# First sequence: when GpSimd rotates k and q, and where blocks of the second layer's weights and the split of k stand in the queues

## The chip, the cores and the metric

The kernel runs on one core of a Trainium2 chip. A core has a matrix engine (TensorE, PE in the profile, with its weight loads as PEld), VectorE (DVE), ScalarE (ACT) and GpSimd (POOL); SyncE (SP) issues most transfers. Each engine works through its own queue in order and waits on semaphores for what others produce. The metric is the device time of one execution, in microseconds; less is better.

## The reference

For eight sequences of 512 rows and 256 columns, with `xn` the layer norm of `x`:

```python
xn = _layernorm(x)
s = attention(xn, in_proj_w, out_proj_w)   # 16 heads of 16, rotary embedding on q and k,
                                           # causal, no further back than 250 positions
h = concatenate([xn, -xn])                 # 512 columns
h = 2 * relu(s0 * (h @ sign(k0)))          # to 1024; sign: True is 1, False is -1
h = 2 * relu(s1 * (h @ sign(k1)))          # to 1024
h = s2 * (h @ sign(k2))                    # to 256
x = x + s * silu(h)
```

The weights of the three layers come as booleans, one byte each; k1 is 1024 x 1024.

## The kernel before, in words

**Work and tiles.** Everything is computed transposed, with the 512 positions of a sequence along the free axis. The two layers take the eight blocks ("units") of 128 features one after the other. To keep precision with fast matrix formats, the input, h1 and h2 are each held as a high half in float16 (ScalarE, L529) and a low half (VectorE, L527: the PSUM result less the high half); a unit's matmuls run over all high blocks and then over all low ones. The PSUM tiles of the units come from a pool of three (`ps_m`), so that a unit can start when the low half of the unit three before it is written. The weights are made from the bytes on the chip: for the second layer a block is one of eight groups of 128 output features, once as float16 (`w1h`) and once as float32 (`w1l`). `make_w1` does it, on ScalarE (L192) or GpSimd (L194). Its source `kb1` is one transfer of 1 MB, which ScalarE's queue issues at 4.33 us and which lands at about 14.7 us.

**q and k.** `project` multiplies the normed input by the weights of q or k, in a part "a" and a part "b" of 512 positions each. VectorE multiplies each by cosine and sine (L404), two instructions to a part; the products of part "b" lie in a tile `m_b` of one buffer, those of "a" in one of two. `rotate` (L425) combines them on GpSimd, two instructions. `split_hi` rounds the result on ScalarE (L442) and sends it to DRAM; `split_lo` takes the rest on VectorE (L449) and sends it too (L435). `stack` (L457) reads them back in the layout of the scores, for a group of four heads at a time: one load for k and two for q. SP issues all of these transfers. The high half lies in one buffer (`hi`).

**v.** `project_v` multiplies for v in four pieces, whose PSUM tiles come from the pool of two that q's projections use before them and the scores behind them (`ps_s`); ScalarE copies each into `v_pad` (L372).

**The order.** `run` is a planner written in the kernel. Each piece of work has a place (`at`) and a cost in planner's units; the pieces are taken by place, and a clock adds up their costs. What follows a piece (the evictions, the rotation, the splits) has a delay, and is issued before the first piece at which the clock has reached its due time. An engine's queue has its instructions in the order of issue. Pieces with a negative place come first. In the first sequence the clock stands at 2.74 before place 0. The halves of k's a and b then cost 0.87 each (to 4.48), q's a and b 1.75 each (to 7.98), the units of the first layer 0.87 each. So k's b products are due at 4.48, q's b products at 7.98 + 1.5 = 9.48, unit 0's eviction at 8.85 and unit 1's at 9.72, the low halves 0.6 later, and v0's copy at 10.59. `rotate` is due 1.4 behind the b products; `hi_after` and `lo_after` (L401) are the delays of `split_hi` and `split_lo` from the same point. A weight block has cost 0 and is issued at its place.

**Downstream.** Behind the first layer come the units of the second layer (eight of them, each in two parts); the first step of the scores stands between units 1 and 2, and then follow steps of exponentials (ScalarE, L752), masks (GpSimd, L768 and L775) and values. The other seven sequences use the same functions with their own places.

Of the kernel before, what the change touches and what calls it, by code (L numbers as in the profile page):

```python
# [34 lines left out]
def tile_attention_times_gated_ffn(  # L35
# [42 lines left out]
    nc = tc.nc  # L78
# [109 lines left out]
    def make_w1(f, p, engine):  # L188

        w, k = w1[p][:, :, ts(f, P)], kb1[:, :, ts(f, P)]  # L190
        if engine is nc.scalar:
            nc.scalar.activation(w, k, AF.Identity, bias=sgnn[:, 1:2], scale=sgn2[:, 1:2])  # L192
        else:
            engine.tensor_scalar(w, k, sgn2[:, 1:2], sgnn[:, 1:2], ALU.mult, ALU.add)  # L194
# [180 lines left out]
    def project(b, what, part, half=None):  # L375

        st = states[b]
        col = E * "qk".index(what) + P * "ab".index(part)
        if b == 0 and what == "q":
            ps = ps_s.tile([P, 2, T], F32, tag="sc", name=f"{what}{part}_ps_{b}")[:, 0]  # L380
        elif half == 1:
            ps = st.pop(part)
        else:
            ps = ps_m.tile([P, T], F32, tag="mm", name=f"{what}{part}_ps_{b}")
            st[part] = ps
        for cols in [slice(0, T)] if half is None else [ts(half, T // 2)]:
            for c in range(EC):
                nc.tensor.matmul(
                    ps[:, cols], wqkv_sb[:, c, ds(col, P)], st["xT"][:, c, cols],
                    start=(c == 0), stop=(c == EC - 1),  # L390
                )
        if half == 0:
            return

        m = turned.tile(
            [P, 2, T], F32, tag=f"m{part}", name=f"m_{what}{part}_{b}",
            bufs=2 if part == "a" else 1,
        )
        st[what, part] = m

        hi_after, lo_after = (4.0, 5.1) if b else (4.5, 5.7) if what == "k" else (5, 6.2)  # L401

        def times(i):
            nc.vector.tensor_tensor(  # L404
                m[:, i], ps, rope_sb[:, i if part == "a" else 1 - i], ALU.mult
            )

        def both():
            times(0)
            times(1)  # L410
            if part == "b":
                return [
                    (1.4, lambda: rotate(b, what)),
                    (hi_after, lambda: split_hi(b, what)),
                    (lo_after, lambda: split_lo(b, what)),
                ]


        return [(1.5 if b == 0 and what + part == "qb" else 0.0, both)]

    def rotate(b, what):
        st = states[b]
        m, n = st[what, "a"], st.pop((what, "b"))
        for i, op in enumerate((ALU.subtract, ALU.add)):
            nc.gpsimd.tensor_tensor(m[:, i], m[:, i], n[:, i], op)  # L425
# [13 lines left out]
    def split_hi(b, what):  # L439
        st = states[b]  # L440
        hi = st["hi"] = turned.tile([P, 2, T], F32R, tag="hi", name=f"{what}h_{b}")
        nc.scalar.copy(hi, st[what, "a"])  # L442
        to_dram(b, what, 0, hi)

    def split_lo(b, what):
        st = states[b]
        m = st.pop((what, "a"))
        lo = m.bitcast(F32R)
        nc.vector.tensor_tensor(lo, m, st["hi"].bitcast(F32), ALU.subtract)  # L449
        to_dram(b, what, 1, lo)  # L450
# [9 lines left out]
    def prepare(b, plain=False):  # L460
# [26 lines left out]
        for what in "kq":  # L487
            for n, part in enumerate("ab"):
                if b == 0 and what == "k" and not plain:

                    out += [
                        (-34.3 if n == 0 else -32.95, 0.87, lambda p=part: project(b, "k", p, 0)),
                        (at["k"] + dp * n, 0.87, lambda p=part: project(b, "k", p, 1)),
                    ]
                else:
                    out.append((
                        at[what] + dp * n, 1.75, lambda w=what, p=part: project(b, w, p),
                    ))
# [497 lines left out]
            (-32.9 if c == 0 else -32.6, 0, lambda c=c: make_w0l(c)),  # L996
        ]
    for w, f, at, engine in (
        ("l", 0, -20, nc.gpsimd), ("l", 1, -19, nc.gpsimd), ("l", 2, 5.1, nc.gpsimd),
        ("h", 0, -17, nc.scalar), ("h", 1, -16, nc.scalar), ("h", 2, 5.2, nc.gpsimd),  # L1000
        ("l", 3, 11.8, nc.gpsimd), ("l", 4, 11.9, nc.gpsimd), ("l", 5, 12.0, nc.gpsimd),
        ("l", 6, 19.3, nc.gpsimd), ("l", 7, 19.4, nc.gpsimd), ("h", 3, 15.2, nc.scalar),
        ("h", 4, 17.0, nc.scalar), ("h", 5, 18.7, nc.scalar), ("h", 6, 20.4, nc.scalar),
        ("h", 7, 22.2, nc.scalar),
    ):
        everything.append((at, 0, lambda f=f, w=w, e=engine: make_w1(f, w, e)))
# [141 lines left out]
```

## Time and profile before

| | us |
|---|---|
| median of 3 runs | 611.47 |
| lowest and highest | 610.42, 612.76 |
| the profiled execution | 612.91 |
| its span | 611.2 |

Mean clock of TensorE in the profiled execution: 0.991 of full speed. Busy shares of the span: PE 98%, PEld 60%, DVE 63%, POOL 50%, ACT 48%; the 16 DMA engines moved 122 GB/s in the mean. Lists of instructions give: start (us), duration (us), engine, source line, operation, output<-inputs, shape, and in brackets the idle time before it and what ended that. Neighbouring instructions of one kind are merged ("x2"), and the duration is then of all. Tables by stretch give the stretch and its length, then the busy time of PE, PEld, DVE, ACT and POOL, the granted clock of TensorE, the DMA engines' mean busy share and GB/s. The rows of the page with 40 digits show tenths in 40 equal slices of the span.

### The profile page before, as it was taken

What the parts mean: (1) busy time and instruction counts of PE and PEld (TensorE: products, weight loads), DVE (VectorE), ACT (ScalarE), POOL (GpSimd) and SP (SyncE); (2) the same over time, 40 slices, a digit from 0 to 9 for tenths busy, and PEclk for the clock granted to TensorE, in tenths of its full rate; (3) what the DMA queues carried; (4) which work ended last, traced back from release to release, by engine and by line L of the source; (5) the groups of instructions that cost most, each with busy time, mean ns of one, the idle gap of its engine ahead of it and who ended that gap; (6) DMA issues with size and microseconds to landing.
All of it is one profiled execution on the core that took longest, in us unless ns stands there. A gap on an engine that the chain in (4) does not pass through costs nothing. (4 is left out here: it accounts for less than half of the span.)

```text
span 611.2 us, 11176 instructions
## 1 busy us (share of the span) xinstructions
PE 596.9 (98%) x4492; PEld 367.7 (60%) x4492; DVE 384.2 (63%) x606; ACT 295.1 (48%) x414; POOL 308.0 (50%) x368
## 2 busy tenths in 40 slices
PE   7899999999999999999999999999999999999994
PEld 5465565556665556555566566655565556667783
DVE  6654736556675584665856658566676557654774
ACT  4576654435544545545354454543554445555421
POOL 2855542346524665336634357245572446627642
PEclk9799999999999999999999999999999999999998
DMA  9371732216322263314333252432533216212201
GB/s 286 144 242 53 276 122 86 87 70 229 117 87 87 97 215 104 120 55 180 131 104 122 79 218 73 148 112 80 207 101 123 89 69 241 70 54 75 83 1 41
DMA packets 38061, 74.51 MB, mean 122 GB/s; under 512 B 5360, under 2 KB 13040, under 8 KB 38000
## 3 DMA queue, kind: packets, MB, share of 16 engines
q1 hardware_dynamic: 35568, 71.48, 34.0%
q10 hardware_dynamic: 2432, 2.23, 1.1%
q8 instruction: 37, 0.61, 0.4%
q14 instruction: 24, 0.20, 0.1%
HBM read 44.30 MB, written 29.39 MB: 121 GB/s over the span
## 5 line engine op out<-in xcount | busy, mean ns | idle before, releaser
L752 ACT ACTIVATE p<-sc 128x1024 f32<-128x1024 f32 (+2 forms) x144 | 138.3, 1013 | 75.5 <-PE sc L733 45.8
L768 POOL TENSOR_SCALAR_AFFINE_SELECT p<-p 128x512 f32<-128x512 f32 x128 | 91.1, 718 | 126.6 <-ACT p L752 126.5
L518 PE MATMUL h_ps<-h1l,w1l_sb 128*128 128x512 f32 (+1 forms) x576 | 146.2, 396 | 0.0
L518 PE MATMUL h_ps<-h1h,w1h_sb 128*128 128x512 f16 (+1 forms) x576 | 123.1, 356 | 0.0
L518 PEld LDWEIGHTS h_ps<-h1l,w1l_sb 128*128 128x128 f32 x576 | 100.2, 188 | 29.5 <-issue 9.2
L529 ACT ACTIVATE h2h<-h_ps 128x512 f16<-128x512 f32 (+1 forms) x72 | 39.5, 548 | 112.3 <-PE h_ps L518 112.3
L518 PEld LDWEIGHTS <-w1h_sb 128*128 128x128 f16 x576 | 51.2, 98 | 58.7 <-issue 17.3
L775 POOL TENSOR_SCALAR_AFFINE_SELECT p<-p 128x512 f32<-128x512 f32 (+1 forms) x96 | 49.7, 517 | 70.9 <-ACT p L752 67.4
L807 PE MATMUL po<-p,v_pad 128*32 128x378 f32 (+4 forms) x1216 | 76.7, 372 | 0.1
L633 DVE RECIPROCAL den<-den 128x256 f32<-128x256 f32 (+1 forms) x32 | 52.5, 1644 | 24.9 <-POOL den L628 24.9
L527 DVE SCALAR_TENSOR_TENSOR h2l<-h_ps,h2h 128x512 fp32r<-128x512 f32 (+1 forms) x72 | 43.7, 608 | 30.9 <-ACT h2h L529 30.9
L733 PEld LDWEIGHTS sc<-q,k 32*128 32x128 f32 x1216 | 44.0, 184 | 29.4 <-issue 21.5
L527 DVE SCALAR_TENSOR_TENSOR h1l<-h_ps,h1h 128x512 fp32r<-128x512 f32 x64 | 42.8, 680 | 29.4 <-ACT h1h L529 29.4
L884 DVE RECIPROCAL S<-S 128x128 f32<-128x128 f32 x64 | 57.5, 920 | 0.1
L733 PE MATMUL sc<-q,k 32*128 32x378 f32 (+4 forms) x1216 | 57.4, 306 | 0.1
L518 PE MATMUL h_ps<-xl,w0l_sb 128*128 128x512 f32 x128 | 53.7, 501 | 0.0
L807 PEld LDWEIGHTS po<-p,v_pad 128*32 128x32 f32 x1216 | 31.7, 109 | 28.7 <-issue 16.6
L529 ACT ACTIVATE h1h<-h_ps 128x512 f16<-128x512 f32 x64 | 38.1, 598 | 22.1 <-PE h_ps L518 22.1
L518 PE MATMUL h_ps<-xh,w0h_sb 128*128 128x512 f16 x128 | 39.8, 393 | 1.1 <-DVE h1l L527 1.1
L301 DVE TENSOR_TENSOR xT<-xT,of_all 128x512 f32<-128x512 f32 x28 | 22.7, 815 | 26.4 <-DMA of_all<-d 26.0
L572 PE MATMUL z_ps<-h2l,w2l_sb 128*128 128x512 f32 (+1 forms) x144 | 36.1, 391 | 0.2 <-DVE h2l L527 0.2
L365 PE MATMUL v_ps<-wqkv_sb,xT 128*128 128x256 f32 x128 | 33.8, 387 | 1.6 <-ACT v_pad L372 1.6
(101 smaller groups left out, 721.5 us busy)
## 6 DMA issues: line engine op xcount, KB each, us to landing
q<-dq SPq DMA_DIRECT2D x64, 256.0 KB, 3.4
dq<-qh SPq DMA_DIRECT2D x16, 512.0 KB, 3.2
dq<-m_qa SPq DMA_DIRECT2D x16, 512.0 KB, 5.5
k<-dk SPq DMA_DIRECT2D x32, 256.0 KB, 2.7
dk<-kh SPq DMA_DIRECT2D x8, 512.0 KB, 3.6
dk<-m_ka SPq DMA_DIRECT2D x8, 512.0 KB, 2.6
x<-in_x_dram SPq DMA_DIRECT2D x30, 128.0 KB, 2.8
xT<-in_x_t_dram SPq DMA_DIRECT2D x7, 512.0 KB, 5.3
```

What stands on the lines that cost most here:

```text
L365: nc.tensor.matmul(v.rearrange("p n s d -> p (n s d)"), st["xT"][:, c, ts(t, P)], wqkv_sb[:, c, 2 * E :], start=(c == 0), stop=(c == EC - 1),)
L518: nc.tensor.matmul(ph, w[p][:, c, ts(f, P)], st[src + p][:, c, cols], start=(k == 0), stop=(k == n - 1),)
L527: nc.vector.scalar_tensor_tensor(lo, ph, 0.0, hi, ALU.max, ALU.subtract)
L529: high = lambda: nc.scalar.activation(hi, ph, AF.Relu)
L572: nc.tensor.matmul(pz, w2[p][:, c, ts(f, P)], st["h2" + p][:, c, cols], start=(c == 0 and p == "h"), stop=(c == NF1 - 1 and p == "l"),)
L633: nc.vector.reciprocal(part, part)
L733: nc.tensor.matmul(sc[r // 2][:, r % 2, ds(off, n)], st["k0", g][row, ts(j, P)], st[f"q{turn}", g][row, ds(j * P + first, n)], start=(turn ...
L752: nc.scalar.activation(p[:, 2 * half : 2 * half + 2, :n], sc[half][:, :, :n], AF.Exp, scale=D ** -0.5,)
L768: nc.gpsimd.affine_select(out=block, in_=block, compare_op=ALU.is_ge, fill=0.0, base=0, pattern=[[0, 4], [1, P]], channel_multiplier=-1,)
L775: nc.gpsimd.affine_select(out=block, in_=block, compare_op=ALU.is_ge, fill=0.0, base=-1, pattern=[[0, 4], [-1, beyond]], channel_multiplier=1,
L807: nc.tensor.matmul(po[32 * r : 32 * r + 32, ds(j * P + first, n)], v_columns(j, g, r), p_[:, r, ds(off, n)], start=(j == 0), stop=(done an ...
L884: nc.vector.reciprocal(part, part)
```

## The change

Two places in the text change. In the first sequence, k's halves are split 0.5 later on the planner's clock, and q's halves 0.4 and 0.8 earlier. Blocks l0 and l1 of the second layer's weights (GpSimd) move from ahead of place 0 to behind q's projections, block l2 and the float16 block h2 (GpSimd) from 5.1 and 5.2 to 10.2 and 10.3, and block h1 (ScalarE) from -16 to 8.6. The other blocks stay.

```diff
-        hi_after, lo_after = (4.0, 5.1) if b else (4.5, 5.7) if what == "k" else (5, 6.2)
+        hi_after, lo_after = (4.0, 5.1) if b else (5.0, 6.2) if what == "k" else (4.6, 5.4)
...
     for w, f, at, engine in (
-        ("l", 0, -20, nc.gpsimd), ("l", 1, -19, nc.gpsimd), ("l", 2, 5.1, nc.gpsimd),
-        ("h", 0, -17, nc.scalar), ("h", 1, -16, nc.scalar), ("h", 2, 5.2, nc.gpsimd),
+        ("l", 0, 4.6, nc.gpsimd), ("l", 1, 4.65, nc.gpsimd), ("l", 2, 10.2, nc.gpsimd),
+        ("h", 0, -17, nc.scalar), ("h", 1, 8.6, nc.scalar), ("h", 2, 10.3, nc.gpsimd),
         ("l", 3, 11.8, nc.gpsimd), ("l", 4, 11.9, nc.gpsimd), ("l", 5, 12.0, nc.gpsimd),
```

## The prediction

> **What bounds the kernel now.** I read the busy shares in 40 slices first, then the busy time by stretch, then each engine's instructions in order of time from 13 to 45 us.
>
> ```profile
> PE   7899999999999999999999999999999999999994
> PEclk9799999999999999999999999999999999999998
> ```
> ```profile
> 20.00:30.00 10.00, 7.36 (x20) 4.58 (x20) 7.57 (x9) 5.38 (x10) 9.02 (x7) 0.66 0.48 188
> ```
> TensorE (PE) carries the end: 98% busy, with one hole behind the start-up, at 20 to 30 us: 7.36 us busy of 10, at a mean clock of 0.66. Time gained there moves everything later forward, if the wait isn't met again. This is how the hole arises (TensorE, GpSimd, ScalarE, VectorE, in that order):
>
> ```profile
> 18.86 0.60 PE L518 MATMUL h_ps<-xh,w0h_sb 128*128 128x512 f16 x2
> 19.11 0.82 PE L518 MATMUL h_ps<-xl,w0l_sb 128*128 128x512 f32 x2
> 21.57 1.13 PE L365 MATMUL v_ps<-wqkv_sb,xT 128*128 128x256 f32 x4 [1.65 <-ACT v_pad L372]
> 23.77 1.01 PE L518 MATMUL h_ps<-xh,w0h_sb 128*128 128x512 f16 x2 [1.06 <-DVE h1l L527]
> ```
> ```profile
> 14.83 2.39 POOL L194 TENSOR_SCALAR w1l_sb<-kb,sgn,sgnn 128x1024 fp32r<-128x1024 uint8 x2 [7.71 <-DMA kb<-in_k_dram]
> 17.18 2.50 POOL L425 TENSOR_TENSOR m_ka<-m_ka,m_kb 128x512 f32<-128x512 f32 x2
> ```
> ```profile
> 19.72 1.04 ACT L442 CAST kh<-m_ka 128x1024 fp32r<-128x1024 f32 x1 [2.20 <-POOL m_ka L425]
> 20.67 0.59 ACT L529 ACTIVATE h1h<-h_ps 128x512 f16<-128x512 f32 x1
> 21.16 0.36 ACT L372 COPY v_pad<-v_ps 128x256 f32<-128x256 f32 x1
> ```
> ```profile
> 19.72 1.29 DVE L404 TENSOR_TENSOR m_qb<-qb_ps,rope_sb 128x512 f32<-128x512 f32 x2 [1.47 <-POOL m_ka L425]
> 20.92 2.19 DVE L449 TENSOR_TENSOR m_ka<-m_ka,kh 128x1024 fp32r<-128x1024 f32 x1
> 23.04 1.87 DVE L527 SCALAR_TENSOR_TENSOR h1l<-h_ps,h1h 128x512 fp32r<-128x512 f32 x3
> ```
> The products for k are there at 15.55 (14.28 + 1.27 on VectorE), but GpSimd is building two weight blocks and rotates k at 17.18 to 19.67. ScalarE stands in front of k's high half meanwhile; behind it in its queue are unit 1's eviction and v0's copy, and TensorE waits for that copy (1.65). VectorE waits too, because m_b has one buffer: q's b products need k's rotated. Then k's low half holds unit 1's low half until 23.73, and unit 4 waits for its PSUM buffer (1.06). In the granted clock's windows the clock falls to 0.50 at 22.96 and is back at 29.79. Units 4, 5, v2 and unit 6 take 23.77 to 30.23 = 6.46 us; at the full clock, by the rows at 15 to 19 us, 0.91 for a unit and 0.87 for a v, 3.60. The clock costs 2.86. Unit 0 of the second layer starts at 32.00. From 19.93 (19.11 + 0.82) to there lie 12.07 us with work for 4 x 0.91 + 3 x 0.87 = 6.25: **5.82 us are lost** (2.71 in gaps, 2.86 by the clock, 0.25 elsewhere).
>
> **The change, step by step** (times of the profiled execution).
>
> *GpSimd.* By the planner's due times, k's rotation comes first, then blocks l0 and l1, then q's rotation, then l2, h2, l3 to l5. Rotation of k: 15.55 to 18.05 (row: 2.50 for two). l0 and l1: to 20.45 (2.39 for two). Nothing is added, only moved. l0 and l1 are needed when the second layer's low pass begins (33.54 before), so they keep over 8 us; l2 and h2 would be done by about 26.4 and serve unit 2, at 40.02 before.
>
> *ScalarE.* Before: h0, h1, unit 0, k high, unit 1, v0, ... The due time of k's high half moves from 8.98 to 9.48 on the planner's clock; unit 1's eviction is due at 9.72, so on ScalarE **the high half still stands ahead of unit 1**, contrary to the words of the change. Only block h1 moves, to between unit 1 and v0. So: h0 14.67 to 15.87; unit 0 at 16.4 (its matmuls end about 16.35) to 17.0; k high 18.1 to 19.1; unit 1 to 19.65; h1 (1.23, from L192's rows) to 20.8; v0 to 21.1; units 2 and 3 at 21.6 and 22.2. Queued behind the moved h1 are v0's copy and every later eviction, and v1 waits for v0's copy: TensorE resumes about 21.15, not 21.57. I take that wait as the trace names it. If v1 in truth waits for q's products (19.35), it starts at 19.93 without a gap.
>
> *VectorE.* Unit 0 low 17.0 to 17.7; q's b products 18.1 to 19.35 (1.29); unit 1 low 19.7 to 20.35, now ahead of k's low half; then k low, then units 2 and 3. k low meets GpSimd: its 2.19 us began under a block that ended at 22.00, and the rotation beside it took 2.24 (the longest of m_qa's rows) where 1.27 is usual. Both fit one taking turns: VectorE waits for GpSimd's running instruction, then runs 1.1 us alone. With l1 ending at 20.45, k low ends at 21.55 if it goes first, or at 22.8 if half a rotation (1.25) goes first; I take 22.2. [...]
>
> *TensorE.* v1 21.15 to 22.0, unit 4 to 22.9. Unit 5 needs unit 2's low half (k low + 0.7): 22.3 to 23.5, so it starts at 22.9 to 23.5. Then 3 x 0.91 + 2 x 0.87 = 4.47: the second layer starts at 27.4 to 28.0, say 27.7, if the clock holds. Gaps: 1.2 + 0 to 0.6. **Gain 32.0 - 27.7 = 4.3.** Unit 0 there needs the buffer of unit 5, whose low half now stands behind q's low half: about 26.9, in time.
>
> *q's path.* Rotation: one row of 2.50 plus 1.1 of taking turns, 20.45 to 24.0 (25.47 before); q high to 25.05 (27.21); q low waits for a block to 25.2 and ends at 26.3 (30.08). SP issues q's high write at 25.05 and the low one at 26.4: 2.2 and 3.7 earlier. Before, the high write occupied the DMA engines from 28.0 to 30.5, ahead of the low one; now they overlap by some 1.1 us. So the last load for step 0 of the scores, issued at 35.02, gains 2.6 to 3.7. It landed at 37.5 to 38.8 (2.5 to 3.8 after issue), and the scores ran at 39.30 without waiting for it. After: 33.8 to 36.2, and TensorE is there at 35.0. I allow 0.1. Behind them the first masks: GpSimd is free after w2, l6 and l7 some 0.2 late, since the moments now follow VectorE's later low halves. Nothing else in the list moves, and PE's slices stay at 9 to the end, so no later cover is spent.
>
> **Sum:** 4.3 - 0.1 - 0.2 = 4.0. Against the profiled execution (612.91 us: span 611.2 and 1.71 around it) that is 608.9. It is the slowest of the four known runs; the median of the others is 611.47, 1.44 below. If that is all the clock's doing (2.86 lost here, perhaps less elsewhere), 608.9 stands, as the loss is gone; if all is a constant offset, 607.5. The runs spread by 2.34, the size of the clock's cost, so I go nearer the first: **608.5**, 0.49% below the median. 0.5% (608.4 to 614.5) is about what a measurement of this kernel can tell from no change.
>
> **The clock.** The window 19.55 to 22.96 was 1.51 us busy of 3.41 (44%) and the clock fell at its end. The next, 76% busy, did not bring it back; a full one did. After the change a window holds 1.2 to 1.8 us of gaps: 47 to 65% busy, between known ends (44% falls; 6 to 9 us, some 85%, holds). I take that it holds, as the mid value is 56%. [...]
>
> **Rivals.**
> 1. *The clock falls all the same.* For: 47% is near 44%. Units 5 to 7 and v2 and v3 at half speed lose up to 2.9, and q's loads are early then: 608.5 + 2.6 = 611.1.
> 2. *v1 doesn't wait for v0's copy.* Then only unit 5's wait is left; the second layer starts at 26.9 to 28.0. About 0.6 better: 607.9. For: q's products end before the copy, and may hold the buffer; against: the row names the copy, which ended 0.05 us ahead.
> 3. *q's loads come late.* The crowded writes let TensorE stand at step 0 for up to 1.2 us: 609.7.
> 4. *Slower.* The same place, worse: if the last load lands over 1.9 us after TensorE is there (after 36.9), the gap is as large as those that halved the clock. With no gain at all it would land at 38.8, 3.8 late. 1.9 to 3.8 of waiting and 2.9 for the clock, less the 0.1 allowed, give 608.5 + 4.7 to 6.6 = 613.2 to 615.1. Against: the load would have to gain under 2 us where its source gains 3.7.
>
> **Chances.** Forecast 0.48, clock 0.20, v1 0.18, q late 0.08, slower 0.06. The forecast's own range, 607.5 to 609.3, lies across 608.4: 0.25 of it is faster by over 0.5%. Faster: 0.25 + 0.16 = 0.41; slower by over 0.5% (the upper part of the last case): 0.03; within: 0.56. The range of 8 in 10 goes from the early v1 with the offset to the clock's case: 606.9 to 611.2.
>
> **What would show it.** GpSimd's rotation of k at 15.55, k high at 18.1 on ScalarE, unit 1's low half ahead of k's: the order. v1's start, with what ended its wait: 21.15 or 19.93. The clock in 20 to 30 us: 1.00, or 0.50 again from a window's end. The second layer's first matmul at 27.7. TensorE idle before the first scores: q late. The forecast is wrong if the second layer starts after 29, or if a hole opens later that wasn't there.

## The result, and the profile after

The changed kernel takes **608.03 us** in the median of 20 runs (607.29 to 611.26), the kernel before 610.92 (609.83 to 612.76, 20 runs beside them). The ratio is 0.9955, with a 95% interval of 0.9947 to 0.9963. The profiled execution of the changed kernel took 608.77 us (span 607.0), that of the kernel before 612.91 (span 611.2).

The hole at 20 to 30 us is nearly gone. The table by stretch of the changed kernel has the same columns as the row shown of before:

```profile
20.00:30.00 10.00, 9.89 (x45) 6.62 (x44) 8.36 (x17) 7.00 (x13) 10.00 (x8) 1.00 0.70 277
```

TensorE is busy 9.89 us instead of 7.36, at the full clock. Next, the engines one by one, in order of time. GpSimd:

```profile
15.41 2.52 POOL L425 TENSOR_TENSOR m_ka<-m_ka,m_kb 128x512 f32<-128x512 f32 x2 [8.39 <-DVE m_kb L404]
17.92 2.38 POOL L194 TENSOR_SCALAR w1l_sb<-kb,sgn,sgnn 128x1024 fp32r<-128x1024 uint8 x2
20.27 3.48 POOL L425 TENSOR_TENSOR m_qa<-m_qa,m_qb 128x512 f32<-128x512 f32 x2
```

k's rotation stands in front of the two blocks and ends at 17.93 instead of 19.68. q's rotation ends at 23.75 instead of 25.47, and its two instructions take 3.48. ScalarE and VectorE:

```profile
17.97 1.05 ACT L442 CAST kh<-m_ka 128x1024 fp32r<-128x1024 f32 x1 [0.62 <-POOL m_ka L425]
18.92 0.59 ACT L529 ACTIVATE h1h<-h_ps 128x512 f16<-128x512 f32 x1
19.41 1.23 ACT L192 ACTIVATE w1h_sb<-kb,sgnn,sgn 128x1024 f16<-128x1024 uint8 x1
20.54 0.36 ACT L372 COPY v_pad<-v_ps 128x256 f32<-128x256 f32 x1
...
23.78 1.05 ACT L442 CAST qh<-m_qa 128x1024 fp32r<-128x1024 f32 x1 [1.08 <-POOL m_qa L425]
```
```profile
19.54 0.69 DVE L527 SCALAR_TENSOR_TENSOR h1l<-h_ps,h1h 128x512 fp32r<-128x512 f32 x1 [0.27 <-ACT h1h L529]
20.15 1.22 DVE L449 TENSOR_TENSOR m_ka<-m_ka,kh 128x1024 fp32r<-128x1024 f32 x1
```

k's high half still stands ahead of unit 1's eviction (17.97 and 18.92; an eviction is ScalarE's instruction that reads a unit's PSUM tile and writes its high half), and block h1 between that and v0's copy. k's low half now takes 1.22 instead of 2.19. TensorE (v1, unit 5, the second layer, the first scores, the masked scores at 48 us):

```profile
20.14 1.02 PE L365 MATMUL v_ps<-wqkv_sb,xT 128*128 128x256 f32 x4
...
22.18 0.59 PE L518 MATMUL h_ps<-xh,w0h_sb 128*128 128x512 f16 x2
...
26.74 1.89 PE L518 MATMUL h_ps<-h1h,w1h_sb 128*128 128x512 f16 x8
...
34.73 0.62 PE L733 MATMUL sc<-q,k 32*128 32x378 f32 x12 [0.27 <-DMA q<-dq]
...
48.65 0.79 PE L733 MATMUL sc<-q,k 32*128 32x378 f32 x14 [0.20 <-ACT p L752]
```

v1 starts without a stated wait, before v0's copy has begun. The second layer starts at 26.74 instead of 32.00. Two new waits stand behind it: the first scores wait for a load of q, and the scores at 48 us for exponentials.

**Where the time went.** To compare two executions free of their start-up I set each matmul beside the one of the same number in the kernel before, and took off the difference at unit 0's first matmul of the first layer. That start lies between 15.21 and 16.24 us in the thirteen other traces, and at 15.27 in before. The table has what is gained (us) at the start of the second layer, behind the first scores, at 56 us, and at the end:

| kernel | second layer | behind first scores | 56 us | end |
|---|---|---|---|---|
| changed | 5.64 | 5.09 | 4.42 | 4.79 |
| 1: only l0, l1 moved | 3.91 | 2.69 | 2.01 | 2.12 |
| 2: only the delays | 3.69 | 3.01 | 2.34 | 2.34 |
| 3: changed, l2 and h2 back | 3.30 | 2.14 | 1.98 | 2.37 |
| 4: changed, h1 back | 5.63 | 5.23 | 4.83 | 5.22 |
| 4 again | 5.62 | 4.94 | 4.25 | 4.57 |
| 5: before, holes filled | 2.99 | 2.98 | 2.58 | 2.71 |
| 6: changed, moments first | 5.53 | 4.99 | 4.99 | 5.41 |
| 6 again | 5.58 | 5.09 | 5.08 | 5.36 |
| 7: changed, q ahead of l0 | 4.93 | 4.94 | 4.77 | 5.04 |
| 8: 6 and 7 together | 4.93 | 4.93 | 4.93 | 5.43 |
| 9: changed, old delays | 5.77 | 5.00 | 4.26 | 4.75 |
| changed again | 5.52 | 4.80 | 4.13 | 4.44 |

In the changed kernel 5.64 are gained at the hole, 0.55 given back at the first scores and 0.67 at 48 us; 0.37 come back by the end, by what was not followed up. The profile of before lost about 2.9 to the clock (0.50 from 22.96 to 29.79), and in none of the others did the clock fall there (1.00 from 18 to 32 us in all thirteen). So, as an estimate from row 5, some 2.7 of each row is the clock's, and the rest the order's.

### The profile page after: what moved, and what is told of

It is laid out like the page before. It is cut to its first block, busy times and chain, and to the rows that moved or that the text cites. A ratio compares the mean times of both kernels' runs of the same rounds, so it can differ in the third digit from the quotient of the medians.

```text
span 607.0 us, 11176 instructions
## 1 busy us (share of the span) xinstructions
PE 594.8 (98%) x4492; PEld 367.2 (60%) x4492; DVE 383.5 (63%) x606; ACT 294.7 (49%) x414; POOL 309.0 (51%) x368
## 5 line engine op out<-in xcount | busy, mean ns | idle before, releaser
L733 PEld LDWEIGHTS sc<-q,k 32*128 32x128 f32 x1216 | 44.2, 184 | 30.4 <-issue 21.1
L518 PE MATMUL h_ps<-xl,w0l_sb 128*128 128x512 f32 x128 | 52.3, 489 | 0.0
L518 PE MATMUL h_ps<-xh,w0h_sb 128*128 128x512 f16 x128 | 38.4, 382 | 0.1
L425 POOL TENSOR_TENSOR m_ka<-m_ka,m_kb 128x512 f32<-128x512 f32 x16 | 20.1, 1276 | 28.5 <-DVE m_kb L404 28.5
```

What stands on the lines that cost most here:

```text
L518: nc.tensor.matmul(ph, w[p][:, c, ts(f, P)], st[src + p][:, c, cols], start=(k == 0), stop=(k == n - 1),)
L733: nc.tensor.matmul(sc[r // 2][:, r % 2, ds(off, n)], st["k0", g][row, ts(j, P)], st[f"q{turn}", g][row, ds(j * P + first, n)], start=(turn ...
```

## The experiments

**My theory at first (A):** GpSimd's order ahead of k's rotation is all; l0 and l1 behind it make the gain. **Rival (B):** a hole is left and the clock falls in it again.

**1. Only l0 and l1 moved** (before, two places changed):

```diff
-        ("l", 0, -20, nc.gpsimd), ("l", 1, -19, nc.gpsimd), ("l", 2, 5.1, nc.gpsimd),
+        ("l", 0, 4.6, nc.gpsimd), ("l", 1, 4.65, nc.gpsimd), ("l", 2, 5.1, nc.gpsimd),
```

> The kernel before, with blocks l0 and l1 alone moved behind k's rotation (places 4.6 and 4.65); l2 and h2 stay at 5.1 and 5.2, so that four blocks now stand ahead of q's rotation, and the splits keep their delays. Theory A (GpSimd's order ahead of k's rotation is the cause of the hole, the rest are details): k's rotation at 15.5, the clock holds at 1.00, the second layer starts at about 27.2 instead of 32.0; but q's rotation starts at about 22.7, its last load for the first scores is as late as before, and TensorE waits there 1.5 to 2.0. Ratio to before 0.9955 to 0.9975. Theory B (the order of the low halves counts as much: with k's low half still ahead of unit 1's, unit 4 waits, and the clock falls all the same): second layer at 29.5 or later, clock 0.50 for some 7 us, ratio 0.999 or more.

Measured: 610.48 us (609.64 to 614.09), ratio 0.999 (0.9974 to 1.0005). Both theories missed: the time is B's and not A's, but the clock was 1.00 in the trace, so B's mechanism is not the reason. ScalarE and TensorE of this run:

```profile
26.12 1.05 ACT L442 CAST qh<-m_qa 128x1024 fp32r<-128x1024 f32 x1 [2.42 <-POOL m_qa L425]
```
```profile
22.01 0.59 PE L518 MATMUL h_ps<-xh,w0h_sb 128*128 128x512 f16 x2 [0.87 <-DVE h1l L527]
...
28.44 1.89 PE L518 MATMUL h_ps<-h1h,w1h_sb 128*128 128x512 f16 x8 [0.93 <-DVE h1l L527]
```

k's rotation was early (15.38) and v1 didn't wait. But unit 4 waits 0.87 for unit 1's low half, which with the old delays stands behind k's (theory B had named that wait). And with l2 and h2 still ahead of q's rotation ScalarE stands 2.42 us in front of q's high half. Behind that in its queue is unit 5's eviction, and the second layer waits for unit 5's low half. The first scores then wait 0.96 for q. What was gained at k is lost at these three places.

**2. Only the delays** (before, L401 as in the change):

> The kernel before, with the delays of the splits alone changed (k 5.0 and 6.2, q 4.6 and 5.4); all weight blocks at their old places. Theory A: k is still rotated at 17.2 to 19.7, so ScalarE and VectorE stand as before; unit 1's low half comes 1.7 earlier, but unit 5 then waits for unit 2's behind k's low half, so that the gaps and the clock's fall stay: ratio 0.999 to 1.001. Theory B: the second wait goes, the clock holds, ratio 0.995 to 0.997.

Measured: 610.35 us (609.15 to 612.06), 0.9991 (0.9979 to 1.0003), the time that theory A had: no difference by itself. But A had also said that both gaps and the clock's fall stay; in the trace the clock held and the second gap was down to 0.16 (at unit 5), as theory B had it. TensorE has the old wait of v1, behind a rotation of k at 16.94:

```profile
21.34 1.13 PE L365 MATMUL v_ps<-wqkv_sb,xT 128*128 128x256 f32 x4 [1.47 <-ACT v_pad L372]
```

**3. l2 and h2 back** (the changed kernel, with q's rotation again behind them):

```diff
-        ... ("l", 2, 10.2, nc.gpsimd),
+        ... ("l", 2, 5.1, nc.gpsimd),
-        ... ("h", 2, 10.3, nc.gpsimd),
+        ... ("h", 2, 5.2, nc.gpsimd),
```

> The changed kernel, with l2 and h2 back ahead of q's rotation (5.1 and 5.2). Theory A: nothing changes up to the second layer's start (26.7 to 27.2, clock 1.00), but q's rotation starts 2.4 later, about 22.7, and the first scores wait for q's last load by 1.5 to 2.5 (0.27 to 0.5 in the changed kernel). Ratio to before 0.9965 to 0.9985. Rival: q's loads have slack that the profile doesn't show, or the wait there is soon made up elsewhere: ratio 0.995 to 0.996, as the changed kernel.

Measured: 610.66 us (609.8 to 611.68), 0.9996 (0.9984 to 1.0008): the whole gain is gone, more than expected. ScalarE and TensorE show why:

```profile
25.71 1.04 ACT L442 CAST qh<-m_qa 128x1024 fp32r<-128x1024 f32 x1 [3.42 <-POOL m_qa L425]
26.66 0.59 ACT L529 ACTIVATE h1h<-h_ps 128x512 f16<-128x512 f32 x1
```
```profile
28.67 1.89 PE L518 MATMUL h_ps<-h1h,w1h_sb 128*128 128x512 f16 x8 [2.31 <-DVE h1l L527]
```

TensorE runs through to 26.36 and then stands 2.31 us. It is experiment 1's wait at q without the one at unit 4: q's high half holds unit 5's eviction. This is a wait that I had not named. Not all of the loss need be that wait: four of the 12 runs (611.36 to 611.68) have a mean clock of 0.994 or 0.995, and the other eight a median of 610.2.

So theory A fell. **Theory C:** the gain is two waits of ScalarE, for k's rotation and for q's, that have to go together; the clock is a small part of it; and the changed kernel gives some back behind the hole, where q's loads and then the statistics of the next sequence stand in SP's queue. (Experiments 1 and 3 leave q's wait and take k's away. No kernel here leaves k's and takes q's away.)

**4. Block h1 back** (the changed kernel, `("h", 1, -16, ...)` instead of 8.6), run twice:

> The changed kernel, with block h1 back ahead of the first eviction on ScalarE (place -16). Theory A: ScalarE builds both blocks until 17.3, unit 0's eviction comes 0.6 later, k's high half stays at 18.0 because it waits for the rotation, and v0's copy comes 0.9 earlier; the second layer starts within 0.3 of the changed kernel's: ratio to before 0.995 to 0.9963. Rival: unit 0's late eviction pushes q's b products and unit 1's low half on VectorE, v1 or unit 4 waits 0.6 to 1.2, and the loss stays: ratio 0.9965 to 0.9975.

> The changed kernel with block h1 ahead of the first units again, as in the earlier run of it (609.15, ratio 0.997, with a profiled execution of 607.58 in which nothing was late). Theory (h1 ahead makes the start hang on the landing of the bytes: with it ScalarE has 2.4 us of blocks before unit 0's eviction and k's high half, so a landing 0.5 us or more later than in that profile delays both): again 608.6 to 609.4 in the median, ratio 0.9965 to 0.998; if the profile has the bytes at 15.3 us or later, unit 0's eviction starts at 17.7 or later and k's high half after it at 18.3, behind the rotation's end. Rival (scatter of that call): 607.8 to 608.4, ratio 0.995 to 0.996.

Measured: 609.15 us (607.48 to 610.73, 12 runs), 0.997 (0.9957 to 0.9982); then 608.45 (608.03 to 609.89, 6 runs), 0.9964 (0.9953 to 0.9976). The first is in the rival's range, though without the wait that the rival named; the second lies between its two expectations. In the traces it does nothing that can be told from scatter: 5.22 and 4.57 gained, 4.79 and 4.44 in those of the changed kernel. In the second trace h0 and h1 begin at 15.03, unit 0's eviction at 17.30 and k's high half, still waiting 0.38 for the rotation, at 18.26. No profile caught a late landing of the weights' bytes, so whether such landings make up the 0.4 us between the medians (608.73 of 18 runs, 608.29 of the 26 of the changed kernel) stays open.

**5. Before, with its holes filled.** What is the clock worth? Idle matmuls on TensorE (they compute nothing that is used) fill the two holes of the old order:

```diff
-        (-31.0, 0, lambda: enough(0)),
+        (-31.0, 0, lambda: enough(0)), (10.5, 0, lambda: warm(8)), (10.8, 0, lambda: warm(5)),
```

> The kernel before, with 13 matmuls that compute nothing used (the identity by itself, into a spare PSUM tile) in TensorE's queue: 8 ahead of v1 and 5 ahead of unit 4, where TensorE stood for 1.65 and 1.06. They fill the gaps and so take the fall of the clock away, and nothing else. Runs of the kernel before so far: 22 of 35 had a mean clock of 0.996 or more, median 610.46; the 13 below it, 611.83. Theory C (the clock is a matter of the run, worth 0.5 in the median; what the change gains is the waits, above all q's loads for the first scores): clock 1.00 from 20 to 30 us, nearly all runs at 0.996 or more, second layer at 29.0 to 29.6, then TensorE waits about 1 for q's last load; ratio 0.9985 to 0.9998. Rival D (the clock is most of the gain, as the profile of before suggests with 2.86 of 5.82): ratio 0.9955 to 0.997.

Measured: 610.38 us (610.25 to 610.94), 0.9992 (0.9982 to 1.0003). TensorE (the 8 and 5 idle matmuls are 16 and 10 rows of the profile):

```profile
20.47 1.95 PE L224 MATMUL warm<-ident 128*128 128x128 f32 x16
...
23.16 1.28 PE L224 MATMUL warm<-ident 128*128 128x128 f32 x10
...
29.72 1.89 PE L518 MATMUL h_ps<-h1h,w1h_sb 128*128 128x512 f16 x8
```

The order is the old one, and the clock held (1.00 in the trace, a mean of 0.996 or more in every run). Against the profile of before that is 2.71 us; in the median it is 0.4 (610.74 for the kernel before, measured beside it), and the interval of the ratio takes in no difference at all. Theory C fits: the fall of the clock is not in every run of the kernel before. Of 35 runs 22 had a mean clock of 0.996 or more, with a median of 610.46; of the changed kernel's 20 runs 18, with a median of 607.94. By this sorting, with the clock held on both sides, the change is worth some 2.5 us. The sorting is rough: the changed kernel's profiled execution has 0.995 with no fall before 601 us, so a mean just under 0.996 need not be a fall in the hole.

**6. The moments ahead of the loads of the second group.** In the changed kernel SP issues the loads of k and q for the scores' second group, and behind them the four small writes of the next sequence's moments, which come back as `of_all`:

```profile
32.51 0.42 SPq L457 DMA_DIRECT2D k<-dk  x1
32.98 0.90 SPq L457 DMA_DIRECT2D q<-dq  x2
33.92 1.36 SPq L281 DMA_DIRECT2D d<-moments  x4
35.38 0.41 SPq L273 DMA_DIRECT2D xT<-in_x_t_dram  x1
38.73 0.34 SPq L290 DMA_DIRECT2D of_all<-d  x1
```

`of_all` goes out 2.94 us behind the end of the issue ahead of it, when the moments have landed (SP's wait for them is 2.5 of that); in the kernel before it was 1.39 (issue of xT at 38.69 for 0.41, `of_all` at 40.49). VectorE then waits for it, and behind VectorE ScalarE's exponentials are late:

```profile
42.62 2.93 DVE L301 TENSOR_TENSOR xT<-xT,of_all 128x512 f32<-128x512 f32 x4 [2.21 <-DMA of_all<-d]
```

The experiment puts the moments first:

```diff
-            if b and g == 1:
-                at = first + 0.01
+            if g == 1:
+                at = first + 0.01 if b else 18.8
```

> The changed kernel, with the loads of the second group of heads of the first sequence (k, q, q) issued behind the second sequence's moments on SP (place 18.8 instead of 17.1), so that the four small writes of the moments and the load that spreads them don't stand behind them. Theory C: 0.65 of the gain was given back at 48 us because that load went out at 38.7 (only 1.8 earlier than before, while TensorE was 5.3 earlier); here it goes out by 36, that wait goes, and the second group's loads are still in time for 44 us. 0.4 to 0.7 faster than the changed kernel: ratio to before 0.994 to 0.995. Rival: the wait at 48 us is made by the masks or the evictions of ScalarE, and the time stays as the changed kernel's, 0.995 to 0.9962.

> The same kernel as the one with the moments' write ahead of the loads of the second group, now beside the changed kernel on one chip. Theory C (the changed kernel gives 0.65 back to SP's queue): of_all issued at 35.2, no wait of the masked scores at 48 us, 0.5 to 1.0 below the changed kernel, near 607.2 and a ratio of 0.994 to 0.9955. Rival (the difference of the earlier call was scatter between chips): within 0.3 of the changed kernel, near 607.8.

> The changed kernel itself, beside the two others. Theory C: 607.9 to 608.3, ratio 0.9955, with v1 at 20.1 without a wait and of_all issued at 38.7. Rival (what the profile showed was one execution's): v1 waits for v0's copy in this execution, 21 us, or of_all goes out before 37.

Measured: 607.21 us (606.95 to 608.37), 0.9949 (0.9935 to 0.9962). Beside the changed kernel on one chip: 607.89 (607.46 to 609.11), 0.9954 (0.9938 to 0.9971), and the changed kernel 608.64 (608.03 to 609.26), 0.996 (0.9945 to 0.9975). SP's queue and the scores at 48 us in the first of these runs:

```profile
32.03 1.37 SPq L281 DMA_DIRECT2D d<-moments  x4
33.45 0.41 SPq L273 DMA_DIRECT2D xT<-in_x_t_dram  x1
35.18 0.34 SPq L290 DMA_DIRECT2D of_all<-d  x1
35.57 0.43 SPq L457 DMA_DIRECT2D k<-dk  x1
```
```profile
47.73 0.80 PE L733 MATMUL sc<-q,k 32*128 32x378 f32 x16
```

`of_all` goes out at 35.18 instead of 38.73, and the scores at 48 us run through. Both traces have 0.6 to 1.0 more at the end than the two of the changed kernel, and the medians lie 0.75 and 0.8 lower. The intervals of the ratios overlap, so the times alone don't show the difference; the traces do, in which the wait is gone twice and there twice. 607.21 is the lowest median here, but of 5 runs, and 7 and 8 lie within the scatter.

**7. q's rotation ahead of l0 and l1** (the changed kernel):

```diff
-        ("l", 0, 4.6, nc.gpsimd), ("l", 1, 4.65, nc.gpsimd), ...
+        ("l", 0, 10.1, nc.gpsimd), ("l", 1, 10.15, nc.gpsimd), ...
```

> The changed kernel, with blocks l0 and l1 behind q's rotation too (10.1 and 10.15). Theory C: q's rotation starts at 19.3 instead of 20.27 and ends about 0.8 earlier although it takes turns with k's low half; the wait of the first scores (0.3 to 0.5) goes, the second layer starts as before this edit (l0 is ready by 24.5, needed at 28.2): 0.2 to 0.5 faster than the changed kernel, ratio to before 0.9945 to 0.9955. Rival: k's low half now waits for the rotation's first instruction, unit 2's low half and unit 5 come 0.3 to 1.2 later, and the time is the changed kernel's or worse: 0.9955 to 0.9975.

Measured: 607.58 us (607.13 to 608.01), 0.9949 (0.9936 to 0.9963). The first scores run without a wait, as the theory had it, and a new gap opens at unit 5, as the rival had it. VectorE and TensorE:

```profile
20.05 2.20 DVE L449 TENSOR_TENSOR m_ka<-m_ka,kh 128x1024 fp32r<-128x1024 f32 x1
```
```profile
22.91 0.59 PE L518 MATMUL h_ps<-xh,w0h_sb 128*128 128x512 f16 x2 [0.95 <-DVE h1l L527]
```

q's rotation runs from 18.65 to 21.17 here, so k's low half meets it and takes 2.20 instead of 1.22; units 2 to 4 have their low halves some 0.8 later.

**8. 6 and 7 together:**

> The edits of the two runs before this one together. Theory C: their gains add, 0.6 to 1.2 faster than the changed kernel, ratio to before 0.9935 to 0.9948. Rival: one limit stands behind the other, and together they give no more than the better one.

Measured: 607.81 us (606.81 to 608.17), 0.995 (0.9936 to 0.9964). Neither wait behind the hole is there, but unit 5's gap (0.95) is: 5.43 at the end, the same as experiment 6 alone. The rival was right, the gains do not add.

**9. The old delays** (the changed kernel with L401 as before):

> The changed kernel with the delays of before, all five blocks as in the change. Only VectorE's queue and SP's change: k's low half again ahead of unit 1's low half, unit 5's low half ahead of q's low half. Theory C (both rotations early are all): unit 4 then waits for unit 1's low half as in the run with l0 and l1 alone (0.87), and the second layer starts 0.6 to 0.9 later than 26.74, while unit 5 is unchanged; q's low write goes out 0.7 later, and the first scores wait 0.6 to 1.2 instead of 0.27. Of 5.26 some 4.4 is left at the second layer, 3.6 behind the first scores: 608.6, ratio 0.9955 to 0.997. Rival (the delays do nothing in the full set, as alone): unit 4 does not wait, 608.0, ratio 0.9945 to 0.996 and a second layer at 26.7.

Measured: 608.41 us (607.58 to 609.06), 0.9955 (0.994 to 0.9971), and the changed kernel beside it 608.64. k's low half goes ahead of unit 1's low half (19.55, 1.26 us long) and unit 4 stands 0.1 at most; unit 5's low half goes ahead of q's, q's low write goes out 1.2 later (27.66 against 26.50 in the second trace of the changed kernel), and the first scores wait 0.51 against 0.48. Theory C's waits did not come; the rival was right: in the full set too, the delays make no difference that can be measured. But the delays and h1's place may cover for each other. Unit 4 waits 0.87 in experiment 1, which has the old delays and h1 at -16 (and l2 and h2 at their old places); it does not in 4, with h1 alone back, nor here, with the delays alone back. The changed kernel with both back was not run.

## Why the prediction was right or wrong

The total was right, 608.9 for the profiled execution against 608.77, and 608.5 for the median against 608.03. Its terms were not all right, and that the total fits so well is in part luck.

- **The order: right.** k's rotation was at 15.41 (15.55 forecast), k's high half at 17.97 (18.1), ahead of unit 1 as the due times gave it; block h1 and v0's copy ended at 20.90 (21.1), q's rotation at 23.75 (24.0), q's low write went out at 26.11 (26.4). All of this in an execution whose start-up was 0.38 later.
- **v1's wait: wrong.** "TensorE resumes about 21.15" failed; it was 20.14, rival 2. The built programs tell why: in the kernel before, v1's first matmul waits on ScalarE, in the changed one on VectorE. Its PSUM buffer is another one. It is VectorE in every program here that has block h1 at 8.6, just ahead of v0's copy (the changed kernel, 3, 6 to 9) and ScalarE in those that have it at -16 (before, 1, 2, 4, 5). In 1 and 4 v0's copy ended at 19.75 and 19.72, so v1 didn't wait there either. Why the pool gives the buffers so wasn't tried. The lesson is in the wrong step: I carried a dependency over from the old trace into a program that was built anew.
- **k's low half: the lower end was right.** I took 22.2, between 21.55 and 22.8; it ended at 21.37. It began before q's rotation, and the rotation paid: 3.48 for two, where k's took 2.52.
- **The second layer: 27.4 to 28.0 forecast, 26.74 measured.** The 1.0 is v1's wait and the mid value for k's low half.
- **The first scores: mis-sized.** 0.1 allowed, 0.55 given back. The loads themselves were in the forecast's span (33.8 to 36.2; TensorE went on at 34.73). TensorE was there 1.0 earlier than forecast (34.02, not 35.0), so half of what the last two points gained was lost here.
- **"No later cover is spent": wrong.** I counted the masks (0.2) and not the moments. They stand behind the loads in SP's queue, and cost 0.67 at 48 us; experiment 6 takes that away.
- **q's side: right in the sum, missed as a cause.** I followed q's rotation only to its loads. Experiment 3 shows that its larger effect is on ScalarE: with q's rotation late, unit 5's eviction holds the second layer up by 2.31. I forecast the gain as one chain from k's rotation; it is two waits. With q's alone left over the gain is gone (0.999 and 0.9996). For k's alone left over there is only an estimate, from the trace of 2: v3's matmuls start there at 27.10 and the next could start 0.86 later, at 27.96. That is 12.75 behind unit 0's start, and the changed kernel has 11.09, so an early q by itself would leave 1.7 at the second layer.
- **The clock: held, as forecast, but not by the forecast's test.** The windows were to be 47 to 65% busy; as v1 didn't wait, none from 17.81 to 28.05 was under 96% (3.41, 3.31 and 3.41 us busy of 3.41). The scale by busy share isn't borne out besides: in experiment 3 a stretch of 3.41 us that was 32% busy held (last section). And I charged 2.86 of the gain to the clock, which left 1.1 of the 4.0 for the order. In the median the clock is worth about 0.4 (experiment 5), and the 2.9 us between the medians are some 2.5 for the order, with the rest for runs in which the clock fell. The forecast had 3.0 between the medians, from a clock's part too large and an order's part too small: that these cancel is luck.
- **Rivals.** 1 did not come (the clock was 1.00 in the hole in all the later profiles). 2 came. 3 came by less than half its price. 4 did not: the last load gained enough.

The terms erred in both directions: 5.26 instead of 4.3 at the second layer (without the correction for the start-up), and 0.55 and 0.67 given back instead of 0.1 and 0.2, 4.04 in all. Two executions of the changed kernel gave 4.79 and 4.44 at the end with the correction, so some 0.35 of any of these sums is scatter.

## What to carry to other kernels

Follow a moved result through the queue of the engine that consumes it: what stands behind the consumer there (here unit 5's eviction behind q's high half) may be worth more than the result itself, and with two such places one repair alone can measure as nothing. An edit that measures as nothing when it alone is taken back may only be covered by another. Where TensorE comes earlier, look at each transfer that it will now meet, small writes behind large loads in one issuing queue first. A wait read in an old trace belongs to that program's buffers: give the case in which it isn't there a real chance when the code is built anew.

## What the runs showed of the hardware

**The clock is a matter of the execution, not only of the order.** In the profile of before the cold spell (0.50) went from 22.96 to 29.79, which is 6.83 us, and the last fall of the clock, at 606.64, is 583.68 behind the first: 85.5 spells, or 171 halves of a spell, of 3.413 each. That the clock moves in such steps, and with that the prediction's windows of 3.41 us, is an estimate from these two distances. The 3.41 us before the first fall were 44% busy (1.51), with a gap of 1.65 in them. The mean clock of 35 runs of that kernel lay between 0.991 and 0.998; seven had 0.994 or less. A gap or a busy share alone doesn't decide it. In experiment 3 TensorE stood 2.31 us, to 28.67, so that the 3.41 us from 26.36 were 32% busy (1.10), and the clock was 1.00 from 24 to 32 us. What makes the difference stays open; that it is where the hole lies in such a step is not shown.

**VectorE and GpSimd: of these instructions the one that started second took longer.** In the changed kernel k's low half, from 20.15, took 1.22 us, and the first instruction of q's rotation, from 20.27, took 2.24, the second 1.28. In experiment 7 k's low half came during a rotation and took 2.20, and the three blocks that GpSimd built next, beside k's and then q's low half, took 5.50 (from 21.14) where three at 27.14 in the changed kernel took 3.54; q's low half took 1.60. In before a mask of 24 columns took 1.21 beside k's low half (at 62.54), and 0.23 at 61.77. The evictions' low halves, which read PSUM and one tile of SBUF, stayed at 0.69 in the changed kernel and in experiment 7. As an estimate, the rows fit that the second waits until the first's instruction has ended: 0.4 to 1.0 more for each, and in experiment 7 first VectorE and then GpSimd paid it. What the two engines share is not shown.
